# Layer 3 of a four-layer convolution stack: products along h one group ahead, modes with channels innermost

## The chip, the cores and the metric

The kernel runs on one core of a Trainium2 chip. The metric is the device time of one execution in microseconds. The kernel before takes 7563.33 us, the median of three runs (7562.54 to 7565.89). The profile shows one other execution, of 7617.3 us with the profiler on; all times within the kernel below are of that execution, counted from its start.

A core has five engines that run side by side: TensorE multiplies matrices and writes to PSUM, VectorE and ScalarE compute elementwise and carry results from PSUM to SBUF, GpSimd does odd jobs and issues DMAs, SyncE issues DMAs. Each runs its own list of instructions in order and waits on semaphores for the others.

## The reference

The input x has 4 batches of 64 channels of 256 x 256, in fp32. Four layers follow, each a residual over a group norm of 32 groups. The first three are a gated convolution block with a patchwise FFT, a 3 x 3 convolution, and a thresholded convolution. The change is in the fourth, layer 3, which multiplies the low Fourier modes by weights:

```python
def _L3_conv_ref(x, weights1, weights2):
    x_ft = jnp.fft.rfft2(x)
    top = jnp.einsum('bixy,ioxy->boxy', x_ft[:, :, :M1, :M2], w1)
    bot = jnp.einsum('bixy,ioxy->boxy', x_ft[:, :, H - M1:, :M2], w2)
    out_ft = out_ft.at[:, :, :M1, :M2].set(top)
    out_ft = out_ft.at[:, :, H - M1:, :M2].set(bot)
    return jnp.fft.irfft2(out_ft, s=(H, W))
...
x = x + _L3_conv_ref(_gn(x), L3_conv_weights1, L3_conv_weights2)
```

M1 and M2 are 16: of 256 x 129 modes only 32 x 16 are kept, so the transforms are small products with cosine and sine matrices.

## The kernel before

Layer 3 (`_layer3`) has two stages. The first computes the kept modes of all batches, scales them by the group norm and multiplies them by the weights. The second transforms back, adds x and stores. The change is in the first.

A batch b is taken in 16 groups of 4 channels (CC). For each group:

1. `load` brings 4 channels of x, 1 MB, into one of six slots (three tags of two buffers, line 1179). A slot is free for the next load when the products of its group are done.
2. Products along h (line 1220, written `psa`): the 256 rows lie as 2 x 128 on the partitions; four matmuls in the code, eight in the trace, give 64 values for each channel and column: 32 frequencies, real and imaginary. Two PSUM tiles (`ps_a`) serve in turn.
3. ScalarE copies the result to SBUF, tile `a` (line 1225; pool `p_a`, three buffers).
4. Four transposes on TensorE (line 1229, `psat`) bring the columns onto the partitions, in one of two PSUM tiles (`ps_t`).
5. VectorE copies them to `ah`, in two operations (line 1235). `ah` is [128, NW, C, 4M]: for each channel the 64 values stand together. There is one buffer of it.

When a batch is complete, products along w (line 1248, `psx`) contract the columns; they read `ah` with the channels 64 words apart. ScalarE copies the result to `xw` (line 1255). TensorE turns it (line 1261, `psxt`) so that channels are on the partitions, and VectorE writes the modes to `xm`, times the group norm's factor r, in 24 operations (lines 1271 to 1273: for each half s of the frequencies and each of 4 strips k, one operation for the upper 64 partitions and two for the lower, where real and imaginary parts change places and one gets a minus). Two small operations (line 1276) add the mean's part to the zero mode. After the last batch the modes are multiplied by the weights (line 1287, `psm`), which wait for all of `xm`.

In layers 0 to 2 the order of TensorE, VectorE, ScalarE and SyncE is that of the program text (`tc.manual_schedule`). Layer 3 is not in such a block. There a planner orders the instructions of each engine at build time: it goes through them with its own estimates of how long each takes, and of those whose inputs and buffers it believes ready it takes the one that stands first in the program. The chip then runs each list as planned, in order. So the program text decides between instructions that are ready together, and the estimates decide what is ready.

Of the kernel before, what the change touches and what calls it, by code (L numbers as in the profile page):

```python
# [10 lines left out]
F32 = mybir.dt.float32  # L11
U32 = mybir.dt.uint32
AF = mybir.ActivationFunctionType
ALU = mybir.AluOpType
# [3 lines left out]
C = 64  # L18
# [100 lines left out]
class _Net:  # L119
# [1044 lines left out]
    def _layer3(self, ctx, src, dst):  # L1164
        tc, nc, a, B, H, W = self.tc, self.nc, self.a, self.B, self.H, self.W
        pool = lambda c, name, bufs, **k: c.enter_context(tc.tile_pool(name=name, bufs=bufs, **k))
        M = MODES
        NH, NW = H // 128, W // 128
        CC, NK = 4, 2
# [3 lines left out]
        def load(b, c0, name, pool=None):  # L1173
            if pool is None:
                x = self.slot(next(turn) % 3, name).rearrange("p r w -> p (r w)")[:, 0 : CC * NH * W]
                x = x.rearrange("p (c n w) -> p c n w", c=CC, n=NH)
            else:
                x = pool.tile([128, CC, NH, W], F32, tag="x", name=name)
            nc.sync.dma_start(
                x.rearrange("p c n w -> p c (n w)"),  # L1180
                src[b][c0 : c0 + CC].rearrange("c (p n) w -> p c (n w)", n=NH),
            )
            return x

        first = {c0: load(0, c0, f"x3_0_{c0}") for c0 in range(0, NX * CC, CC)}
        cp = pool(ctx, "l3c", 1)
        eh = self.load("c_eh", cp)
        ew = cp.tile([128, NW, 2, 2 * M], F32, name="ew")
# [4 lines left out]
        xm = cp.tile([128, 2, M, M, 2, B], F32, name="xm")  # L1193

        om = cp.tile([128, M, B, 3, M], F32, name="om")
        halves = [slice(0, C), slice(C, 128)]

        with ExitStack() as c2:
            p_w = pool(c2, "l3w", 3)
            p_ah, p_a = pool(c2, "l3ah", 1), pool(c2, "l3a", 3)  # L1200
            ps_a, ps_t = pool(c2, "l3pa", 2, space=PSUM), pool(c2, "l3pt", 2, space=PSUM)
            ps_x, ps_m = pool(c2, "l3px", 1, space=PSUM), pool(c2, "l3pm", 1, space=PSUM)
            wts, xs = {}, {}
            self.small = lambda name: ps_m.tile([128, 512], F32, tag="m", name=name)

            def load_w(k0):
                wt = wts[k0] = p_w.tile([128, 2, NK, M * C], F32, tag="w", name=f"wt_{k0}")
                nc.sync.dma_start(wt, a["wf"][:, :, k0 : k0 + NK])

            for b in range(B):  # L1210

                ah = p_ah.tile([128, NW, C, 4 * M], F32, tag="ah", name=f"ah_{b}")
                for c0 in range(0, C, CC):
                    x = first.pop(c0, None) if b == 0 else None
                    x = xs[b, c0] = x or load(b, c0, f"x3_{b}_{c0}")
                    for c1 in range(0, CC, 4):
                        ps = ps_a.tile([128, 2, W], F32, tag="a", name=f"psa_{b}_{c0}_{c1}")
                        for n in range(NH):
                            for j in range(2):
                                nc.tensor.matmul(  # L1220
                                    ps[halves[j]], eh[:, n, :], x[:, c1 + 2 * j : c1 + 2 * j + 2, n, :],
                                    start=(n == 0), stop=(n == NH - 1),
                                )
                        m = p_a.tile([128, 2, W], F32, tag="m", name=f"a_{b}_{c0}_{c1}")
                        nc.scalar.copy(m, ps)  # L1225
                        pt = ps_t.tile([128, NW, 2, 2, 4 * M], F32, tag="t", name=f"psat_{b}_{c0}_{c1}")
                        for n in range(NW):
                            for k in range(2):
                                nc.tensor.transpose(  # L1229
                                    pt[:, n, k].rearrange("p j f -> p (j f)"),  # L1230
                                    m[:, k, n * 128 : (n + 1) * 128], self.ident,
                                )
                        c = c0 + c1
                        for n in range(NW):
                            nc.vector.tensor_copy(
                                ah[:, n, c : c + 4, :].rearrange("p (j k) f -> p k j f", j=2), pt[:, n]
                            )
                    if c0 % 16 == 0:
                        self.next_norms()
                if b < 3:  # L1240
                    load_w(b * NK)

                psx = ps_x.tile([128, 4, 128], F32, tag="x", name=f"psx_{b}")
                ahv = ah.rearrange("p n c (s g k r) -> p n g r k s c", s=2, g=4, k=4)
                for n in range(NW):
                    for ri in range(2):
                        for g in range(4):
                            nc.tensor.matmul(  # L1248
                                psx[32 * g : 32 * g + 32].rearrange("p k (s c) -> p k s c", s=2),
                                ew[:, n, ri, :], ahv[:, n, g, ri],  # L1250
                                start=(n == 0 and ri == 0), stop=(n == NW - 1 and ri == 1),
                                tile_position=(0, 32 * g),
                            )
                xw = p_a.tile([128, 4, 128], F32, tag="m", name=f"xw_{b}")
                nc.scalar.copy(xw, psx)

                pxt = ps_x.tile([128, 2, 4, 4, 2, M], F32, tag="xt", name=f"psxt_{b}")
                for s in range(2):
                    for k in range(4):
                        for h in halves:  # L1260
                            nc.tensor.matmul(
                                pxt[h, s, k].rearrange("p g r w -> p (g r w)"), xw[:, k, s * C : (s + 1) * C],
                                self.ident, start=True, stop=True,
                            )
                r, nb = self.r[3][:, b : b + 1], self.nb[3][:, b : b + 1]
                up, low = halves
                for s in range(2):
                    xb = xm[:, s, :, :, :, b].rearrange("p (g k) w r -> p k g w r", g=4)
                    for k in range(4):
                        v = pxt[:, s, k].rearrange("p g r w -> p g w r")  # L1270
                        nc.vector.tensor_scalar(xb[up, k], v[up], r[up], None, ALU.mult)
                        nc.vector.tensor_scalar(xb[low, k, :, :, 0], v[low, :, :, 1], r[low], -1.0, ALU.mult, ALU.mult)
                        nc.vector.tensor_scalar(xb[low, k, :, :, 1], v[low, :, :, 0], r[low], None, ALU.mult)
                for k, h in enumerate(halves):
                    dc = xm[h, 0, 0, 0, k, b : b + 1]
                    nc.vector.scalar_tensor_tensor(dc, nb[h], float(H * W), dc, ALU.mult, ALU.add)

            for k0 in range(0, M, NK):
                if k0 + 2 * NK < M and k0 > 0:
                    load_w(k0 + 2 * NK)  # L1280
                wt = wts[k0]
                ps = ps_a.tile([128, 2, W], F32, tag="a", name=f"psm_{k0}").rearrange("p k w -> p (k w)")
                ps = ps[:, 0 : NK * M * 2 * B].rearrange("p (k w r b) -> p k w r b", k=NK, w=M, r=2)
                for k in range(NK):
                    for kw in range(M):
                        for s in range(2):
                            nc.tensor.matmul(
                                ps[halves[s], k, kw].rearrange("p r b -> p (r b)"),
                                wt[:, s, k, kw * C : (kw + 1) * C],
                                xm[:, s, k0 + k, kw].rearrange("p r b -> p (r b)"), start=True, stop=True,  # L1290
                            )
                for k in range(NK):
                    nc.scalar.copy(om[:, :, :, 0:2, k0 + k], ps[:, k].rearrange("p w r b -> p w b r"))
                    nc.vector.tensor_scalar(om[:, :, :, 2, k0 + k], ps[:, k, :, 0, :], -1.0, None, ALU.mult)

        with ExitStack() as c2:
            p_x2, p_z, p_tm = pool(c2, "l3x2", NY), pool(c2, "l3z", 3), pool(c2, "l3t", 2)
            ps_t, ps_z = pool(c2, "l3pt2", 2, space=PSUM), pool(c2, "l3pz", 2, space=PSUM)
# [19 lines left out]
            for i, (b, c0) in enumerate(parts):  # L1318
# [3 lines left out]
                if i < NX:  # L1322
                    x = xs[b, c0]
                else:
                    x = load(b, c0, f"x4_{b}_{c0}", p_x2 if (i - NX) % (NX + NY) < NY else None)
# [53 lines left out]
```

## Time and profile before

| what | value |
|---|---|
| time, median of 3 | 7563.33 us |
| profiled span | 7617.3 us |
| first psa to last psxt of layer 3 | 6976.7 to 7232.7 us |
| products along w start (batches 0 to 3) | 7040.4, 7100.5, 7160.1, 7222.9 us |
| products with the weights (psm) | 7241.3 to 7296 us |
| second stage of layer 3 | to the end |
| psa matmuls, 512 of them | mean 624 ns |
| copy to `a`, 64 | mean 586 ns |
| psat transposes, 256 | mean 290 ns |
| copy to `ah`, 128 | mean 419 ns |
| operations to `xm`, 96 | mean 456, 340, 337 ns |

In the profile PE is TensorE (PEld its loading of weights), DVE VectorE, ACT ScalarE, POOL GpSimd and SP SyncE. A row of the timeline reads: start, length, engine, line, operation, tile written <- tiles read, shape, count, and in brackets how long the engine was idle before it and what ended that. Matmuls overlap in the engine, so a duration is longer than the pace at which they follow each other; the pace is read from their starts. The windows view gives busy time and count of each engine in a stretch, then the granted clock of TensorE (1.00 is full), the busy share of the DMA engines and their GB/s.

### The profile page before, as it was taken

How to read it: one execution, taken by the hardware profiler on the slowest of the kernel's cores; microseconds unless marked ns; L12 is line 12 of the kernel's file. 1: busy time of each engine (PE TensorE's matmuls, PEld its weight loads, DVE VectorE, ACT ScalarE, POOL GpSimd, SP SyncE). 2: the span in 40 equal slices, each digit the busy share in tenths (PEclk: the TensorE clock that was granted, in tenths of full speed). 3: DMA queues.
4: the chain of work that ended last, by engine and by line, in shares of the span. 5: the costliest groups of instructions: out<-in, count | busy, mean ns of one | idle time of the engine just before them, and what ended most of it. 6: DMA issues, size and time to landing. Idle time of an engine off the chain costs nothing. (4 is left out here: it accounts for less than half of the span.)

```text
span 7617.3 us, 398890 instructions
## 1 busy us (share of the span) xinstructions
PE 7303.1 (96%) x189304; PEld 4319.0 (57%) x189304; DVE 6594.7 (87%) x5915; ACT 3659.3 (48%) x3917; POOL 660.3 (9%) x1435
## 2 busy tenths in 40 slices
PE   6999999999999999999999999899989999998797
PEld 4666666666666666666666666433324444443276
DVE  7999999999999999999899899899989888885345
ACT  3445444444444454444444545322238778774111
POOL 0000000000000000000000000001102222221011
PEclk9999999999999999999999999999999999999955
DMA  3222222222222222222111121487766766677789
GB/s 129 62 65 63 63 61 61 59 61 59 61 62 61 59 59 62 62 59 54 45 47 47 46 50 44 100 197 196 195 162 171 178 171 175 171 178 232 243 333 396
DMA packets 651203, 875.63 MB, mean 115 GB/s; under 512 B 44020, under 2 KB 470212, under 8 KB 647524
## 3 DMA queue, kind: packets, MB, share of 16 engines
q1 hardware_dynamic: 568548, 581.61, 28.8%
q0 software_dynamic: 81024, 268.50, 12.1%
q8 instruction: 1485, 24.33, 1.4%
q14 instruction: 146, 1.20, 0.1%
HBM read 581.50 MB, written 268.44 MB: 112 GB/s over the span
## 5 line engine op out<-in xcount | busy, mean ns | idle before, releaser
L462 PE MATMUL psd<-y,diag 32*32 32x512 f32 x73296 | 2547.8, 598 | 16.0 <-issue 14.5
L500 DVE SCALAR_TENSOR_TENSOR v<-y,sb_w_dw,v 128x2048 f32<-128x2048 f32 x1024 | 2391.0, 2335 | 110.3 <-ACT v L498 87.7
L462 PEld LDWEIGHTS psd<-y,diag 32*32 32x32 f32 x73296 | 1524.3, 103 | 877.9 <-issue 366.7
L442 ACT COPY y<-psy 128x512 f32<-128x512 f32 x1536 | 915.4, 659 | 1683.3 <-PE psy L435 1681.2
L400 DVE TENSOR_TENSOR up<-psu,flt 128x768 f32<-128x768 f32 x1024 | 932.4, 951 | 226.6 <-PE psu L397 225.8
L435 PEld LDWEIGHTS psy<-sb_c_bdft,up 64*64 64x64 f32 x49152 | 859.5, 135 | 350.9 <-issue 139.1
L435 PE MATMUL psy<-sb_c_bdft,up 64*64 64x64 f32 x49152 | 931.3, 221 | 32.6 <-issue 29.7
L397 PE MATMUL psu<-win,xf 64*64 64x384 f32 x8192 | 788.5, 487 | 18.5 <-DVE h L482 10.1
L1000 DVE TENSOR_TENSOR q<-xn 128x2313 f32<-128x2313 f32 (+2 forms) x256 | 627.3, 2493 | 1.7 <-ACT xn L236 1.7
L1055 PE MATMUL one<-z,wp 32*32 32x512 f32 x16384 | 592.6, 596 | 20.3 <-issue 15.4
L1001 ACT ACTIVATE q<-q 128x2313 f32<-128x2313 f32 (+2 forms) x256 | 528.9, 2086 | 32.0 <-DVE q L1000 30.7
L476 ACT ACTIVATE h<-psd 128x1024 f32<-128x1024 f32 x258 | 251.3, 1023 | 534.9 <-PE psd L462 534.9
L236 ACT ACTIVATE xn<-x,nb,r 128x1024 f32<-128x1024 f32 (+3 forms) x272 | 488.1, 1798 | 41.5 <-DVE q L1000 23.6
L1055 PEld LDWEIGHTS one<-z,wp 32*32 32x32 f32 x16384 | 366.5, 103 | 228.5 <-issue 87.4
L1014 PE MATMUL div<-q,ones 64*32 64x512 f32 x8192 | 469.0, 597 | 13.6 <-ACT q L1001 9.8
L407 POOL MEMSET y<- 128x22 f32 x384 | 52.2, 137 | 4251.2 <-ACT y L415 3217.2
L397 PEld LDWEIGHTS psu<-win,xf 64*64 64x64 f32 x8192 | 305.6, 134 | 184.6 <-issue 85.2
L1088 POOL DMA_DIRECT2D x<-r x512 | 274.2, 543 | 971.0 <-DVE r L1085 943.6
L809 PE MATMUL m<-t,wk 64*64 64x512 f32 x3072 | 352.5, 588 | 0.0
L809 PE MATMUL m<-t,wg 64*64 64x512 f32 x3072 | 343.5, 591 | 4.5 <-DVE wg L771 4.5
L1014 PEld LDWEIGHTS div<-q,ones 64*32 64x32 f32 x8192 | 153.6, 107 | 321.1 <-issue 256.9
L824 ACT COPY s<-m 128x1024 f32<-128x1024 f32 x64 | 64.8, 1013 | 558.9 <-PE m L809 548.6
(138 smaller groups left out, 7625.2 us busy)
## 6 DMA issues: line engine op xcount, KB each, us to landing
x<-x SPq DMA_DIRECT2D x240, 640.0 KB, 6.3
x<-x SPq DMA_DIRECT2D x122, 1024.0 KB, 10.7
x<-in_x_dram SPq DMA_DIRECT2D x256, 256.0 KB, 3.8
x<-o POOLq DMA_DIRECT2D x128, 512.0 KB, 9.2
r<-x SPq DMA_DIRECT2D x512, 128.0 KB, 4.1
x<-r POOLq DMA_DIRECT2D x512, 128.0 KB, 4.0
out_dram<-x POOLq DMA_DIRECT2D x64, 1024.0 KB, 9.8
r<-in_x_dram SPq DMA_DIRECT2D x248, 256.0 KB, 3.8
```

Source lines behind the costliest of these rows:

```text
L236: self.nc.scalar.activation(dst, src, AF.Identity, bias=self.nb[n][p0:p1, b : b + 1], scale=self.r[n][p0:p1, b : b + 1])
L397: nc.tensor.matmul(ps[halves[n], s, 0:384], xf[t][halves[s], n, 4 * g + k], win[halves[s]], start=True, stop=True)
L400: nc.vector.tensor_mul(ups[t, g][:, :, k, :], ps[:, :, 0:384], flt.broadcast_to([128, 2, 384]))
L435: nc.tensor.matmul(ps[halves[c], n, s, :, k, :], up[halves[n], s, k, i * 128 + c * C : i * 128 + (c + 1) * C], bdft[halves[n]], start=True ...
L442: nc.scalar.copy(yt[t][i][:, 3:11, w0 : w0 + 64].rearrange("p r (k n w) -> p n r k w", k=4, n=2), ps[:, :, s])
L462: ins = nc.tensor.matmul(d[q // 2][quarters[j], q % 2], diag[quarters[q], i, k, :], rows_in(t, i, quarters[q], j, dy)[:, :, dx : dx + W], ...
L500: nc.vector.scalar_tensor_tensor(v, s, wdw[:, 2, k : k + 1], v, ALU.mult, ALU.add)
L809: nc.tensor.matmul(rows2(m)[halves[j], s], gs[i][halves[s], dx, :], ts[n][halves[s], i, 2 * j : 2 * j + 2, dx : dx + W], start=(dx == 0), ...
L1000: nc.vector.tensor_sub(d, p0, p1)
L1001: nc.scalar.activation(d, d, AF.Square)
L1014: ins = nc.tensor.matmul(ps[quarters[j], h], ones[halves[h]], q[n, g, k][halves[h], r + 2 * j : r + 2 * j + 2, o : o + W], start=(m == 0), ...
L1055: ins = nc.tensor.matmul(rows2(ps[g])[quarters[j], k], w[quarters[i]], z[quarters[i], h, 2 * j + dy : 2 * j + dy + 2, dx : dx + W], tile_p ...
```

## The change

The loop over batches becomes three functions and a loop over all 64 groups. `along_h` does steps 1 to 3 of a group, `turned` steps 4 and 5, `along_w` the products along w, `spread` the rest. In each turn i of the loop, `along_h` of group i is given ahead of `turned` of group i − 1. When group i − 1 is the first of a batch, `along_w` of the batch before stands between the two, and `spread` follows `turned`. Its purpose is that TensorE has products to do while ScalarE copies.

`ah` becomes [128, NW, 4M, C], with channels innermost, so that the products along w read neighbouring words; VectorE's copies write with a step of 64 words instead. In PSUM the turned modes are laid out with the strips k inside g, so that one operation can take all four strips: six operations for a batch in place of 24. The weight loads `load_w` come one group earlier in the program. What is computed stays the same.

```diff
-            for b in range(B):
-                ah = p_ah.tile([128, NW, C, 4 * M], F32, tag="ah", name=f"ah_{b}")
...
-                        for n in range(NW):
-                            nc.vector.tensor_copy(
-                                ah[:, n, c : c + 4, :].rearrange("p (j k) f -> p k j f", j=2), pt[:, n]
-                            )
+            ah_of = lambda b: ahs[b].rearrange("p n (s g k r) c -> p n g r k s c", s=2, g=4, k=4)
+            def along_h(b, c0):
...
+            def turned(b, c0):
+                if c0 == 0:
+                    ahs[b] = p_ah.tile([128, NW, 4 * M, C], F32, tag="ah", name=f"ah_{b}")
...
+                for n in range(NW):
+                    nc.vector.tensor_copy(
+                        ahs[b][:, n, :, c0 : c0 + 4].rearrange("p f (j k) -> p k j f", j=2), pt[:, n]
+                    )
...
-                pxt = ps_x.tile([128, 2, 4, 4, 2, M], F32, tag="xt", name=f"psxt_{b}")
+                pxt = ps_x.tile([128, 2, 4, 4, 2 * M], F32, tag="xt", name=f"psxt_{b}")
...
-                                pxt[h, s, k].rearrange("p g r w -> p (g r w)"), xw[:, k, s * C : (s + 1) * C],
-                                self.ident, start=True, stop=True,
+                                pxt[h, s, :, k], xw[:, k, s * C : (s + 1) * C], self.ident, start=True, stop=True
...
-                    xb = xm[:, s, :, :, :, b].rearrange("p (g k) w r -> p k g w r", g=4)
-                    for k in range(4):
-                        v = pxt[:, s, k].rearrange("p g r w -> p g w r")
-                        nc.vector.tensor_scalar(xb[up, k], v[up], r[up], None, ALU.mult)
-                        nc.vector.tensor_scalar(xb[low, k, :, :, 0], v[low, :, :, 1], r[low], -1.0, ALU.mult, ALU.mult)
-                        nc.vector.tensor_scalar(xb[low, k, :, :, 1], v[low, :, :, 0], r[low], None, ALU.mult)
+                    xb = xm[:, s, :, :, :, b]
+                    v = pxt[:, s].rearrange("p g k (r w) -> p (g k) w r", r=2)
+                    nc.vector.tensor_scalar(xb[up], v[up], r[up], None, ALU.mult)
+                    nc.vector.tensor_scalar(xb[low, :, :, 0], v[low, :, :, 1], r[low], -1.0, ALU.mult, ALU.mult)
+                    nc.vector.tensor_scalar(xb[low, :, :, 1], v[low, :, :, 0], r[low], None, ALU.mult)
...
+            groups = [(b, c0) for b in range(B) for c0 in range(0, C, CC)]
+            for i in range(len(groups) + 2):
+                if i < len(groups):
+                    along_h(*groups[i])
+                b, k = divmod(i - 1, NG)
+                if b > 0 and k == 0:
+                    along_w(b - 1)
+                if 0 < i <= len(groups):
+                    turned(*groups[i - 1])
+                if b > 0 and k == 0:
+                    spread(b - 1)
+                if i % NG == NG - 1 and i // NG < 3:
+                    load_w(i // NG * NK)
```

More of the change, by code (lines that the diff above doesn't have):

```diff
@@ L1208, in load_w @@
                 nc.sync.dma_start(wt, a["wf"][:, :, k0 : k0 + NK])
-            for b in range(B):
-                ah = p_ah.tile([128, NW, C, 4 * M], F32, tag="ah", name=f"ah_{b}")
[L1213 to L1222, printed above, removed]
-                                )
-                        m = p_a.tile([128, 2, W], F32, tag="m", name=f"a_{b}_{c0}_{c1}")
-                        nc.scalar.copy(m, ps)
-                        pt = ps_t.tile([128, NW, 2, 2, 4 * M], F32, tag="t", name=f"psat_{b}_{c0}_{c1}")
-                        for n in range(NW):
[L1228 to L1235, printed above, removed]
-                                ah[:, n, c : c + 4, :].rearrange("p (j k) f -> p k j f", j=2), pt[:, n]
[L1237 to L1241, printed above, removed]
@@ new lines, in _layer3 @@
+            NG = C // CC
+            ahs, ms, xws = {}, {}, {}
+            ah_of = lambda b: ahs[b].rearrange("p n (s g k r) c -> p n g r k s c", s=2, g=4, k=4)
+            def along_h(b, c0):
+                x = first.pop(c0, None) if b == 0 else None
+                x = xs[b, c0] = x or load(b, c0, f"x3_{b}_{c0}")
+                ps = ps_a.tile([128, 2, W], F32, tag="a", name=f"psa_{b}_{c0}")
+                for n in range(NH):
+                    for j in range(2):
+                        nc.tensor.matmul(
+                            ps[halves[j]], eh[:, n, :], x[:, 2 * j : 2 * j + 2, n, :],
+                            start=(n == 0), stop=(n == NH - 1),
+                        )
+                m = ms[b, c0] = p_a.tile([128, 2, W], F32, tag="m", name=f"a_{b}_{c0}")
+                nc.scalar.copy(m, ps)
@@ new lines, in turned @@
+            def turned(b, c0):
+                if c0 == 0:
+                    ahs[b] = p_ah.tile([128, NW, 4 * M, C], F32, tag="ah", name=f"ah_{b}")
+                m = ms.pop((b, c0))
+                pt = ps_t.tile([128, NW, 2, 2, 4 * M], F32, tag="t", name=f"psat_{b}_{c0}")
+                for n in range(NW):
+                    for k in range(2):
+                        nc.tensor.transpose(
+                            pt[:, n, k].rearrange("p j f -> p (j f)"), m[:, k, n * 128 : (n + 1) * 128], self.ident
+                        )
+                for n in range(NW):
+                    nc.vector.tensor_copy(
+                        ahs[b][:, n, :, c0 : c0 + 4].rearrange("p f (j k) -> p k j f", j=2), pt[:, n]
+                    )
+                if c0 % 16 == 0:
+                    self.next_norms()
@@ L1243, in _layer3, with along_w @@
+            def along_w(b):
                 psx = ps_x.tile([128, 4, 128], F32, tag="x", name=f"psx_{b}")
-                ahv = ah.rearrange("p n c (s g k r) -> p n g r k s c", s=2, g=4, k=4)
                 for n in range(NW):
@@ L1249, in _layer3 @@
                                 psx[32 * g : 32 * g + 32].rearrange("p k (s c) -> p k s c", s=2),
-                                ew[:, n, ri, :], ahv[:, n, g, ri],
+                                ew[:, n, ri, :], ah_of(b)[:, n, g, ri],
                                 start=(n == 0 and ri == 0), stop=(n == NW - 1 and ri == 1),
@@ L1253, in _layer3, with spread @@
                             )
-                xw = p_a.tile([128, 4, 128], F32, tag="m", name=f"xw_{b}")
+                xw = xws[b] = p_a.tile([128, 4, 128], F32, tag="m", name=f"xw_{b}")
                 nc.scalar.copy(xw, psx)
-                pxt = ps_x.tile([128, 2, 4, 4, 2, M], F32, tag="xt", name=f"psxt_{b}")
+            def spread(b):
+                xw = xws.pop(b)
+                pxt = ps_x.tile([128, 2, 4, 4, 2 * M], F32, tag="xt", name=f"psxt_{b}")
                 for s in range(2):
```

## The prediction

> **What bounds the kernel now.** I read the page first: TensorE is busy 96% of the span, but that is a mean over four layers. The change touches layer 3, the last 640 us, so I went on to the waits between 6972 and 7250 us (engine and line, what it waited for, total us, times, longest).
>
> ```profile
> ACT a L1225 <- PE psa L1220: 167.3, 62, 5.2
> DVE ah L1235 <- PE psat L1229: 131.7, 54, 4.7
> PEld psat L1229 <- ACT a L1225: 96.0, 59, 2.4
> PE psat L1229 <- ACT a L1225: 43.5, 57, 2.3
> DVE xm L1271 <- PE psxt L1261: 39.1, 4, 10.0
> ```
>
> ScalarE and VectorE wait for TensorE, and TensorE waits 57 times (43.5 us) for ScalarE's copy. No row has TensorE waiting for a DMA: the loads keep up. One group of four channels in the timeline (start us, us, engine, line) shows the loop:
>
> ```profile
> 7003.08 0.66 PE L1229 MATMUL psat<-sb_c_ident,a 128*128 128x128 f32 x4 [0.72 <-ACT a L1225]
> 7003.66 0.20 PEld L1220 LDWEIGHTS psa<-x,sb_c_eh 128*64 128x64 f32 x4 [0.17 <-issue]
> 7003.66 1.94 PE L1220 MATMUL psa<-x,sb_c_eh 128*64 128x512 f32 x8
> 7003.77 0.76 DVE L1235 COPY ah<-psat 128x256 f32<-128x256 f32 x2 [2.49 <-PE psat L1229]
> 7005.69 0.59 ACT L1225 COPY a<-psa 128x512 f32<-128x512 f32 x1 [2.66 <-PE psa L1220]
> 7006.32 0.66 PE L1229 MATMUL psat<-sb_c_ident,a 128*128 128x128 f32 x4 [0.72 <-ACT a L1225]
> ```
>
> It is a chain of products, copy, transposes with almost nothing of the next group in the gap: 7003.08 to 7006.32 is 3.24 us a group. The last batch's end is a second serial stretch:
>
> ```profile
> 7222.91 7.06 PE L1248 MATMUL psx<-ah,ew 128*32 128x512 f32 x32 [0.52 <-DVE ah L1235]
> 7230.08 0.59 ACT L1255 COPY xw<-psx 128x512 f32<-128x512 f32 x1 [8.40 <-PE psx L1248]
> 7230.72 1.97 PE L1261 MATMUL psxt<-sb_c_ident,xw 128*64 128x128 f32 x32 [0.75 <-ACT xw L1255]
> 7232.74 0.43 DVE L1271 TENSOR_SCALAR xm<-psxt,r 64x128 f32<-64x128 f32 x1 [9.55 <-PE psxt L1261]
> 7240.83 0.34 DVE L1276 SCALAR_TENSOR_TENSOR xm<-nb,xm 64x1 f32<-64x1 f32 x2
> 7241.32 20.87 PE L1287 MATMUL psm<-xm,wt 128*64 128x8 f32 x388 [8.63 <-DVE xm L1276]
> ```
>
> TensorE stands still 8.63 us while VectorE scales the modes. Last, what the loads could do at most, in three stretches of the windows view (clock, DMA share and GB/s are the last columns; the first two are the steady loop and the stage after, where loads and stores run together):
>
> ```profile
> 7112.00:7160.00 48.00, 38.02 (x182) 14.18 (x182) 18.29 (x54) 8.79 (x15) 0.00 (x0) 1.00 1.01 348
> 7340.00:7350.00 10.00, 8.65 (x51) 6.56 (x43) 6.35 (x11) 1.21 (x2) 1.51 (x2) 0.50 1.04 415
> 7100.00:7112.00 12.00, 11.27 (x75) 3.36 (x74) 1.92 (x7) 1.17 (x2) 0.00 (x0) 1.00 0.27 97
> ```
>
> A DMA share near 1 is not yet the limit: 348 GB/s and 415 GB/s both read as full. While psx runs (third row), the DMA nearly stops because all six slots of x are full. The 3.25 us at which loads are issued is TensorE's pace.
>
> [...] the psa matmuls start two at a time every 0.43 us, so eight take 1.71 us. [...] in the trace it falls in the 8.63 us gap (1.00 until 7234, 0.50 from 7235). [...] the L1235 copies take 419. [...] L1271 takes 440 ns for 128 elements and L1272 340 for 64 (medians), 1.56 ns an element where dense rows take 1.04 (681 ns for 512 on L1345, 1214 for 1024 on L482).
>
> **The change, part by part.**
>
> *Order of products and transposes.* The products along h of group i+1 now stand ahead of the transposes of group i. Nothing of this stage is in a hand-ordered block, so a planner decides; it goes by program order among what it believes ready. It already ran ahead where it could: in the trace two psa matmuls of the following batch stand ahead of psx, and after a psx a run of 20 psa matmuls goes before transposes. So I expect psa(i+1), psat(i), psa(i+2) on TensorE. The buffers allow it: psa has two PSUM tiles and the copy of group i−1 is long done; the copied tile has three; the loads have six slots. The copy's 0.59 us plus its hand-overs then lie beside 1.71 us of products. A group costs 1.71 + 0.58 (from the first transpose to the next psa, 7003.08 to 7003.66) = 2.29 us instead of 3.24, with 0.95 saved.
>
> A batch: 16 x 2.29 + 6.83 (32 psx matmuls at 213.5 ns) + 1.75 (psxt) = 45.2 us. Before, psx starts at 7040.4, 7100.5, 7160.1 and 7222.9, so batches take 60.1, 59.6 and 62.8: savings 14.9, 14.4 and 17.6. The first batch gains less: ScalarE's first copy waits until 6989.2 whatever the order (the idle there is put down to a DMA, 24.0 us), the clock is half until 6996, and psx now has one more group's products in front: about 11 us. Sum 57.9.
>
> *Can the loads follow?* TensorE would ask 1 MB each 2.29 us, 458 GB/s, more than was ever held. Behind a 2 MB weight load at 7139 the trace has loads landing every 2.61 us (five spacings between 7155 and 7168). A batch needs 16 x 2.61 = 41.8 us of transfer within its 45.2. Starting with six full slots, 36.6 us of groups consume 16 and bring 13 or 14, so some 3 stay in hand, which psx refills. Three weight loads of 2 MB cost 5.2 us each, two slots' worth: tight, with some 2 us lost over the stage. I also allow 2 us for hand-overs that I don't see: 57.9 − 4 = about 54 us, with 57 at best.
>
> *Modes with channels innermost.* The psx matmuls now read c at step 1 instead of 64 words, but they already start at 213.5 ns[...]: nothing gained. The L1235 copies now write every element 256 bytes from the last. No row shows this copy; L1294[...] takes 266 ns against 159 for the two-element copies, 1.74 ns an element. So a copy costs between 419 (no penalty) and 158 + 256 x 1.74 = 603 ns. I take 600: 1.2 us of VectorE a group within 2.29, and behind psx's data only at the batch's end, where the next group's 1.71 us of products hides it. Only in the last batch are 0.4 us exposed.
>
> *6 operations for 24.* Now the 24 and two small ones take 8.4 us from the first start to the last end (7232.74 to 7241.17). Then, per s, one of 512 elements and two of 256. At 1.56 ns an element and the intercept of the two rows (240 ns): 1040 + 2 x 640, twice, plus 0.3 = 4.9 us. At 1.04 ns: 770 + 2 x 506, twice, plus 0.3 = 3.9. I take 4.6: 3.8 us saved in the last batch, where psm waits for it. In the first three it lies beside products and only frees VectorE sooner. The strip order in PSUM (32-word pieces) costs psxt nothing I can see: 1.75 us is the weight loads' pace. [...] psm still runs at half clock.
>
> *Moved:* weight loads one group earlier, the norm steps with the transposes: both off the path.
>
> Sum: 54 + 3.8 + 2 of small relief after each psx (VectorE holds the first transposes of batches 1 to 3 for about 0.7 us) = 60 us. The stage after is limited by its transfers (415 GB/s, share 1.04), but these begin only once psm is done and its space is free, so it moves forward whole. 7563.3 − 60 = 7503 us.
>
> **The rivals.**
>
> *Loads bind.* For it: share about 1 in the steady loop, and a landing median of 7.0 us, 5.2 at least. If three in flight sustain only 350 GB/s, 3.0 us a load, a batch is 48 us of loads plus weights, and the saving falls to about 40 + 4: 7519. Against: 2.61 us under backlog.
>
> *The planner keeps its order.* If it thinks x late, transposes still go first, and only the 6-for-24 and the relief remain, some 6 us: 7557. Against: the two matmuls it already puts ahead.
>
> *Slower.* If the 256-byte writes cost 1.8 us a copy, two are 3.6 us a group and VectorE sets the pace: 64 x 0.36 = 23 us more, 7586. The same comes out if the transposes land straight behind their own products, with the 0.43 us that now hides part of the copy lost: 64 x 0.43 − 4 = 23. Against: no strided row above costs over 1.74 ns an element.
>
> **How the numbers follow.** Main case 0.73, loads bind 0.15, order kept 0.07, slower 0.05. The forecast is the main case. The range 7490 to 7528 holds it with copies free of penalty and no stall (lower end) and the loads at 3.0 us (upper end with some 9 us over), and leaves out the last two. Faster by over 0.2% (15 us): 0.73 + 0.15 = 0.88; within: 0.07; slower: 0.05.
>
> **What would show it.** In the profile after: psat not waiting for ACT a any more; groups every 2.3 us; psx starts some 45 us apart; psa waiting for a DMA only for single microseconds; ah copies near 600 ns; six operations a batch in xm's three lines and the gap ahead of psm near 5 us. Wrong if groups stay at 3.2 us (order), or if they sit at 2.6 to 3.0 with waits for x (loads), or if VectorE is busy throughout (writes).

## The result and the profile after

The changed kernel takes 7531.81 us (median of four runs, 7522.21 to 7539.59) where the kernel before takes 7564.61 (four runs, 7562.54 to 7572.59): a ratio of 0.9954, with a 95% interval of 0.9937 to 0.9971. It is faster, by 33 us. The forecast was 60 us (7503), with a range up to 7528 that misses the result by 4 us.

I call *the stage* the stretch from the first psa to the first psm, the part that the change touches. It was 264.6 us (6976.7 to 7241.3) and is 228.6 (6917.9 to 7146.5): 36.0 us less. Layers 0 to 2 are the same program and yet differ from one execution to the next (layer 3 begins at 6976.7 and at 6917.9 in these two), so the stage is the sharper measure below. From the first psm to the end it is 376.0 us before and 374.0 after.

The windows view of the kernel after, cut at the four starts of psx and at the first psm (stretch, us, busy us and count of PE, PEld, DVE, ACT and POOL, granted clock, DMA share, GB/s):

```profile
6917.90:6970.60 52.70, 47.29 (x211) 17.95 (x211) 24.19 (x49) 9.27 (x16) 5.29 (x10) 0.88 1.03 385
6970.60:7024.80 54.20, 47.12 (x258) 17.69 (x256) 21.48 (x40) 9.95 (x17) 0.00 (x0) 1.00 0.95 326
7024.80:7077.90 53.10, 45.36 (x250) 17.22 (x248) 21.04 (x40) 9.95 (x17) 0.00 (x0) 1.00 0.95 332
7077.90:7134.60 56.70, 45.54 (x256) 17.23 (x256) 21.50 (x41) 9.85 (x17) 0.00 (x0) 1.00 0.62 224
7134.60:7146.50 11.90, 5.61 (x64) 2.69 (x65) 5.29 (x9) 0.58 (x1) 0.00 (x0) 0.96 0.01 2
```

Batches 1 to 3, forecast at 45.2 us, last 54.2, 53.1 and 56.7. TensorE is busy only 45 to 47 us of each, and the last batch has a DMA share of 0.62: it isn't the loads that fill it. The waits of the same kernel say what does (engine and line, what it waited for, us, times, longest):

```profile
PEld psat L1236 <- ACT a L1226: 58.1, 40, 2.1
PE psat L1236 <- ACT a L1226: 27.6, 40, 2.0
PEld psat L1236 <- issue: 21.3, 26, 0.9
```

The transposes still wait for ScalarE's copy 40 times; 26 times only their weight load waits, for nothing that the profile shows ("issue"). Counted in TensorE's timeline, 25 of the 64 groups run in the intended order, with the next group's products ahead of their transposes. The timeline shows both kinds. In batch 0:

```profile
6954.24 0.65 PE L1236 MATMUL psat<-sb_c_ident,a 128*128 128x128 f32 x4
6954.41 0.58 ACT L1226 COPY a<-psa 128x512 f32<-128x512 f32 x1 [1.87 <-PE psa L1221]
6954.83 1.94 PE L1221 MATMUL psa<-x,sb_c_eh 128*64 128x512 f32 x8
6956.69 0.42 PEld L1236 LDWEIGHTS psat<-sb_c_ident,a 128*128 128x128 f32 x4 [0.81 <-issue]
6956.70 0.66 PE L1236 MATMUL psat<-sb_c_ident,a 128*128 128x128 f32 x4
```

and in batch 2:

```profile
7053.10 0.58 ACT L1226 COPY a<-psa 128x512 f32<-128x512 f32 x1 [2.68 <-PE psa L1221]
7053.74 0.66 PE L1236 MATMUL psat<-sb_c_ident,a 128*128 128x128 f32 x4 [0.74 <-ACT a L1226]
7054.32 1.94 PE L1221 MATMUL psa<-x,sb_c_eh 128*64 128x512 f32 x8
7056.36 0.58 ACT L1226 COPY a<-psa 128x512 f32<-128x512 f32 x1 [2.68 <-PE psa L1221]
7057.00 0.66 PE L1236 MATMUL psat<-sb_c_ident,a 128*128 128x128 f32 x4 [0.74 <-ACT a L1226]
```

In batch 0 the copy ends (6954.99) long before the transposes that read it (6956.70), with a group of products between: a group each 2.46 us (6954.24 to 6956.70). In batch 2 each copy is followed at once by its own transposes: 3.26 us (7053.74 to 7057.00), as before the change. The planner goes back to the old order within each batch, though the program text does not: the intended order holds for the first 14 groups of batch 0, for the first 5 of batch 1, for the first 5 of batch 2, and for one group of batch 3.

The end of the last batch, in the same timeline:

```profile
7134.65 3.64 PE L1252 MATMUL psx<-ah,ew 128*32 128x512 f32 x32 [0.68 <-DVE ah L1240]
7138.69 0.58 ACT L1259 COPY xw<-psx 128x512 f32<-128x512 f32 x1 [5.43 <-PE psx L1252]
7139.33 1.97 PE L1268 MATMUL psxt<-sb_c_ident,xw 128*64 128x128 f32 x32 [1.04 <-ACT xw L1259]
7141.35 1.11 DVE L1276 TENSOR_SCALAR xm<-psxt,r 64x512 f32<-64x512 f32 x1 [6.32 <-PE psxt L1268]
7146.02 0.34 DVE L1281 SCALAR_TENSOR_TENSOR xm<-nb,xm 64x1 f32<-64x1 f32 x2
7146.50 1.74 PE L1308 MATMUL psm<-xm,wt 128*64 128x8 f32 x29 [5.21 <-DVE xm L1281]
```

The 32 psx matmuls take 3.64 us where they took 7.06, and the gap ahead of psm is 5.21 where it was 8.63.

### The profile page after: what moved, and what is told of

It is laid out like the page before. It is cut to its first block, busy times and chain, and to the rows that moved or that the text cites. A ratio compares the mean times of both kernels' runs of the same rounds, so it can differ in the third digit from the quotient of the medians.

```text
span 7520.5 us, 398811 instructions
## 1 busy us (share of the span) xinstructions
PE 7250.4 (96%) x189304; PEld 4323.5 (57%) x189304; DVE 6598.8 (88%) x5843; ACT 3655.1 (49%) x3917; POOL 659.1 (9%) x1435
## 5 line engine op out<-in xcount | busy, mean ns | idle before, releaser
L1001 ACT ACTIVATE q<-q 128x2313 f32<-128x2313 f32 (+2 forms) x256 | 529.1, 2086 | 32.7 <-DVE q L1000 31.2
```

Of the source, the lines that this page charges most:

```text
L1001: nc.scalar.activation(d, d, AF.Square)
```

## The experiments

My theory after the result, **the order**: the planner reckons with the loads of x coming late, puts a group's own transposes ahead of products that it believes not ready, and so gives back most of the gain; the transfers themselves could follow. The rival, **the transfers**: x arrives too slowly, so a better order would only wait for x. The runs of the first table are from one chip, where the kernel before takes 7599.08 us, those of the second from another, where it takes 7584.31; the last, of the copies alone, is on its own.

| kernel | time, us | stage, us | batches 0 to 3, and the end, us |
|---|---|---|---|
| before | 7599.08 (profile of 7617.3) | 264.6 | 63.7, 60.1, 59.6, 62.8, 18.4 |
| order by hand | 7545.81 | 207.1 | 57.2, 49.3, 46.7, 42.1, 11.8 |
| channels innermost alone | 7583.64 | 252.4 | 63.5, 57.3, 56.8, 59.8, 15.0 |
| order alone, by hand | 7571.63 | 233.4 | 56.5, 55.8, 52.7, 49.8, 18.6 |
| six operations alone | 7599.75 | 263.5 | 62.9, 61.8, 61.4, 62.4, 15.0 |

| kernel | time, us | stage, us | batches 0 to 3, and the end, us |
|---|---|---|---|
| the changed kernel again | 7559.11 | 230.4 | 54.4, 54.3, 53.1, 56.8, 11.8 |
| half the loads, planner | 7523.29 | 199.4 | 54.6, 45.2, 45.3, 42.6, 11.7 |
| half the loads, by hand | 7516.72 | 198.3 | 54.8, 44.8, 44.9, 42.1, 11.7 |
| by hand, weights last | 7517.62 | 199.5 | 56.0, 44.8, 44.8, 42.2, 11.7 |

Times of kernels without an interval below are single runs, and say little: on the first chip eleven runs of the kernel before lie between 7581.48 and 7607.44. A stage is that of one traced execution each. The two traces of the changed kernel show how far it can be trusted: 228.6 and 230.4 us, with the whole difference in batch 0 (52.7 and 54.4), while batches 1 to 3 and the end agree to 0.1 us. A batch here ends where its psx starts (starts rounded to 0.1 us), so a batch's psx and operations to `xm` count in the next column. By hand batch 0 is a little longer than the planner's (56.0 against 54.4); I did not follow that up.

### The order by hand

```diff
+            by_hand = tc.manual_schedule(
+                engines={
+                    mybir.EngineType.PE, mybir.EngineType.DVE, mybir.EngineType.Activation, mybir.EngineType.SP
+                }
+            )
+            with by_hand:
-            for i in range(len(groups) + 2):
+                for i in range(len(groups) + 2):
...
```

> The changed kernel with its loop over groups in a block ordered by the program text, so that each group's products along h stand ahead of the transposes of the group before in all four batches. Measure: time from the first psa to the first psm in the trace (before 264.6 us, changed kernel 228.6 us), and the whole time. Theory O (the planner, taking x for late, put the transposes straight behind their own products in most of batches 1 to 3, and that is what the gain lacks): groups of 2.45 us throughout, batches about 45 us, stage about 200 us, whole time about 28 us under the changed kernel's 7532, near 7504. Rival L (the chip's loads would not have kept up anyway): TensorE waits for x in batches 1 to 3, batches of 50 us or more, stage 215 us or more, whole time within 12 us of the changed kernel's.

The same instructions, in the order of the program text: 7545.81 us (six runs, 7532.46 to 7551.71), ratio 0.9932 (0.9919 to 0.9945). The stage is 207.1 us, 21.5 less than in the changed kernel and 57.5 less than before. The 207.1 are 7 us more than theory O expected (about 200), with batches of 49.3, 46.7 and 42.1 where it had about 45, and well under the 215 of rival L; by the ratios to the kernel before (0.9932 and 0.9954) the whole time gains some 17 us on the changed kernel, where 28 were expected. The block fixes the order of VectorE, ScalarE and SyncE along with that of TensorE; they weren't tried apart. All groups but the last one have the intended order now: 62 times only the transposes' weight load waits, for nothing that the profile shows. So the transfers could follow, nearly. What they cost is in the second of these rows of its waits:

```profile
PEld psat L1236 <- issue: 52.0, 62, 1.6
PE psa L1221 <- DMA x<-x: 5.7, 4, 2.8
```

### Channels innermost alone

```diff
-                ah = p_ah.tile([128, NW, C, 4 * M], F32, tag="ah", name=f"ah_{b}")
+                ah = p_ah.tile([128, NW, 4 * M, C], F32, tag="ah", name=f"ah_{b}")
...
-                                ah[:, n, c : c + 4, :].rearrange("p (j k) f -> p k j f", j=2), pt[:, n]
+                                ah[:, n, :, c : c + 4].rearrange("p f (j k) -> p k j f", j=2), pt[:, n]
...
-                ahv = ah.rearrange("p n c (s g k r) -> p n g r k s c", s=2, g=4, k=4)
+                ahv = ah.rearrange("p n (s g k r) c -> p n g r k s c", s=2, g=4, k=4)
```

> The kernel before with nothing of the change but the channels innermost in ah (order, 24 operations and PSUM strips as before). Theory S (the step of 64 words in the moving operand halved the pace of the psx matmuls): psx takes about 3.6 us in place of 7.0 in each batch, stage 264.6 - 4 x 3.4 = 251 us; the copies to ah take 600 ns in place of 419 and cost under 1 us in all. Rival I (psx only looks shorter in the changed kernel because it is dealt out between psa matmuls): psx stays at 7.0 us, stage 264 to 266 us.

The stage is 252.4 us, 12.2 less than before, and the groups by line show where it comes from (group, shape and count, busy us and mean ns of one, idle before). Of the kernel before:

```profile
L1248 PE MATMUL psx<-ah,ew 128*32 128x512 f32 x128 | 28.2, 1034 | 1.0 <-DVE ah L1235 1.0
```

and with the new `ah` alone:

```profile
L1248 PE MATMUL psx<-ah,ew 128*32 128x512 f32 x128 | 14.6, 595 | 1.4 <-DVE ah L1235 1.4
```

128 matmuls take 14.6 us instead of 28.2, which is 13.6 us over the stage, or 3.4 a batch, and batches 1 to 3 and the end are each some 3 us shorter (2.8, 2.8, 3.0 and 3.4). Only the layout of what they read differs. Theory S had it so: 3.6 us a batch and a stage of 251 us were expected.

### The order alone, by hand

The order by hand, with the old `ah` and the 24 operations.

```diff
-            ah_of = lambda b: ahs[b].rearrange("p n (s g k r) c -> p n g r k s c", s=2, g=4, k=4)
+            ah_of = lambda b: ahs[b].rearrange("p n c (s g k r) -> p n g r k s c", s=2, g=4, k=4)
...
-                    xb = xm[:, s, :, :, :, b]
+                    xb = xm[:, s, :, :, :, b].rearrange("p (g k) w r -> p k g w r", g=4)
+                    for k in range(4):
...
```

> The order by hand as in the first run, but ah with the 64 values innermost, the PSUM strips and the 24 operations as before. If the order is worth what theory O says and adds to the layout: groups of 2.45 us, psx of 7.0 us, batches of 48 to 49 us, a gap of 8.6 us ahead of psm, stage 200 + 4 x 3.4 + 4 = 218 us. If VectorE's 8.4 us of operations behind each psx hold up the transposes once the order is tight: 3 us more a batch, 227 us. If loads bind: no faster than 225 us with TensorE waiting for x.

The stage is 233.4 us, above the 218 and the 227 that were expected. It is also over the 225 of the rival that the loads bind, but TensorE's products wait for x only 4.5 us in all, less than by hand with all three parts (5.7). The order by itself brings 31.2 of the 57.5 that the three parts bring by hand. Against the run with all three, batches 1 to 3 are 6.5, 6.0 and 7.7 us longer. The slower psx is 3.4 of each. For the remaining 2.6 to 4.3 the waits have a row that the run with all three hasn't, one stop of TensorE in each of batches 1 to 3 (the waits for x fall differently in the two runs, so the difference isn't the price of the stop alone):

```profile
PE psat L1236 <- DVE ah L1240: 8.5, 3, 2.8
```

The first of the three in the timeline, after a psx:

```profile
7034.43 0.32 DVE L1283 SCALAR_TENSOR_TENSOR xm<-nb,xm 64x1 f32<-64x1 f32 x2
7034.76 1.41 DVE L1240 COPY ah<-psat 128x256 f32<-128x256 f32 x4
7035.66 1.09 PE L1236 MATMUL psat<-sb_c_ident,a 128*128 128x128 f32 x4 [2.82 <-DVE ah L1240]
7036.68 3.68 PE L1221 MATMUL psa<-x,sb_c_eh 128*64 128x512 f32 x8
```

VectorE is at the 24 operations and the two small ones for 8.5 us (7026.27 to 7034.75); both psat tiles are full until it copies them; TensorE stands 2.82 us, and then a group of products takes 3.68 us instead of 1.94: the granted clock is 0.50 from 7035.7 to 7041.3, by the windows view. The stop of batch 3 (2.82 us, until 7144.16) is followed by slower products too, 3.25 us for the group; that of batch 2 (2.81 us, until 7091.43) is not, and its group takes 1.94. With groups one ahead, this hold of VectorE (8.5 us) stops TensorE.

### Six operations alone

```diff
-                pxt = ps_x.tile([128, 2, 4, 4, 2, M], F32, tag="xt", name=f"psxt_{b}")
+                pxt = ps_x.tile([128, 2, 4, 4, 2 * M], F32, tag="xt", name=f"psxt_{b}")
...
-                    for k in range(4):
...
+                    nc.vector.tensor_scalar(xb[up], v[up], r[up], None, ALU.mult)
+                    nc.vector.tensor_scalar(xb[low, :, :, 0], v[low, :, :, 1], r[low], -1.0, ALU.mult, ALU.mult)
+                    nc.vector.tensor_scalar(xb[low, :, :, 1], v[low, :, :, 0], r[low], None, ALU.mult)
```

> The kernel before with nothing of the change but the six operations for 24 and the PSUM strips that they need. Expected: the gap ahead of psm falls from 8.63 to about 5.2 us (the three lines took 1132, 693 and 664 ns in the changed kernel), 3.4 us of the stage, and 0 to 2 us more from transposes that wait less behind each psx: stage 259 to 261 us. Rival: nothing beyond the gap, and the planner's order shifts: 264 us or more.

The end is 3.4 us shorter, as expected, and yet the stage is 263.5 us, above the expected 259 to 261: it loses only 1.1 us, since batches 1 and 2 are 1.7 and 1.8 us longer. TensorE in the timeline of the kernel before, after its first psx:

```profile
7055.01 0.66 PE L1229 MATMUL psat<-sb_c_ident,a 128*128 128x128 f32 x4 [0.72 <-ACT a L1225]
7055.60 4.59 PE L1220 MATMUL psa<-x,sb_c_eh 128*64 128x512 f32 x20
7060.12 1.18 PE L1229 MATMUL psat<-sb_c_ident,a 128*128 128x128 f32 x8
```

and with the six operations:

```profile
7037.09 0.66 PE L1229 MATMUL psat<-sb_c_ident,a 128*128 128x128 f32 x4 [0.72 <-ACT a L1225]
7037.68 1.94 PE L1220 MATMUL psa<-x,sb_c_eh 128*64 128x512 f32 x8
7040.34 0.65 PE L1229 MATMUL psat<-sb_c_ident,a 128*128 128x128 f32 x4 [0.72 <-ACT a L1225]
```

The 20 products in a row, then 8 transposes without a wait, were a piece of the good order that the planner had found by itself; they stand where VectorE is at its 24 operations (until 7059.1, and until 7037.9 with the six). With the six the planner puts the transposes first, and the wait of 0.72 us returns. That it does so because it reckons with VectorE free sooner is my reading.

### Half the loads, in the planner's hands and by hand

Every second group reads the x of the group before, apart from the last six groups (and the first six, whose loads are given earlier), so that half of the loads of x are left out in batches 1 and 2, and 26 of the 64 in all. The same edit in the changed kernel and in the one by hand:

```diff
+                if c0 // CC % 2 and (b, c0) not in [(B - 1, c) for c in range(C - NX * CC, C, CC)]:
+                    x = x or xs[b, c0 - CC]
                 x = xs[b, c0] = x or load(b, c0, f"x3_{b}_{c0}")
```

> The changed kernel in the planner's hands, but every second group of four channels takes the x of the group before it instead of loading its own, so half of layer 3's loads along h are left out (the output is of other data). Theory P (the planner puts the transposes straight behind their own products because it reckons with x arriving late): with half the loads it has no such reason, the products of the next group stand ahead all through, groups take 2.45 us in every batch, and the first products to the first mode product take about 200 us (228.6 after). Theory L (the transfers themselves keep the groups slow): also about 200 us, but then the run by hand with half the loads is as far below the run by hand with all of them. Theory R (another reason for the planner's order: buffers, priorities): the order stays mixed, groups of 3.26 us remain in batches 1 to 3, about 222 to 228 us.

> The order by hand, with the same half of the loads left out. In the run by hand with all loads some 8 us of waits for x were left in the 207.1 us from the first products to the first mode product. Theory P (the order, not the transfers, held the changed kernel back): about 199 us, only those 8 us less. Theory L (the transfers held it back): much less than 199 us, 190 or under, since then the groups of 2.45 us would also shrink towards 2.29.

In the planner's hands the stage falls from 230.4 to 199.4 us, by hand to 198.3. The planner now keeps the intended order in 63 of 64 groups; its timeline of TensorE in batch 2:

```profile
7057.26 0.65 PE L1238 MATMUL psat<-sb_c_ident,a 128*128 128x128 f32 x4
7057.84 1.94 PE L1223 MATMUL psa<-x,sb_c_eh 128*64 128x512 f32 x8
7059.71 0.66 PE L1238 MATMUL psat<-sb_c_ident,a 128*128 128x128 f32 x4
7060.30 1.94 PE L1223 MATMUL psa<-x,sb_c_eh 128*64 128x512 f32 x8
```

Groups of 2.45 us, no wait for a copy. So what made it leave that order was the loads. And by hand, leaving these loads out is worth only 207.1 − 198.3 = 8.8 us: that is what the transfers cost there, while the planner's order costs 228.6 − 207.1 = 21.5. What the planner takes a load to last isn't in any profile; since each x then also stands in its slot for two groups, "the loads" is here the loads together with the slots that they fill. Nor was the planner's order tried with more slots, or with the loads of weights elsewhere.

### The weights last

```diff
-                    if i % NG == NG - 1 and i // NG < 3:
-                        load_w(i // NG * NK)
+                    if i == len(groups) - 1:
+                        for k0 in range(0, 3 * NK, NK):
+                            load_w(k0)
```

> The order by hand, with the three first weight loads of 2 MB given after the last load of x instead of one at the end of each of the first three batches. Theory W (each weight load makes the x behind it land about 5 us later, and that is the waits for x left in the run by hand): those waits, some 8 us, go; the first products to the first mode product take about 200 us instead of 207, and the ratio to the kernel before is about 0.9923 (0.9932 by hand without this). Theory N (the waits come from the pace of the x loads alone, 2.65 us against 2.45): nothing gained or 2 us at most, 0.9930; and if the weights come too late, psm waits for them and it is slower than that.

> The changed kernel itself on the chip of these runs, so that the versions by hand are compared with it and not only with the kernel before: 0.9954 of the time before, and 0.002 to 0.003 above the version with the weights last if theory P and W hold; no difference beyond 0.001 if the order by hand was worth nothing.

By hand with the weights last: 7517.62 us (four runs, 7513.37 to 7524.32), ratio 0.9909 (0.9894 to 0.9924). The changed kernel in the same runs: 7559.11 (five runs), 0.9964 (0.9951 to 0.9976). The intervals lie apart, by 0.0055 where 0.002 to 0.003 was expected: some 40 us, of which 30.9 are the stage and the rest lies outside it, unexplained. Of the kernels timed in several runs and with all loads this one is the best; against the order by hand with the weights between (0.9919 to 0.9945) the intervals overlap, so that the weights' part is shown by the stage and the waits, not by the time. Its windows:

```profile
7002.80:7047.60 44.80, 44.63 (x258) 17.12 (x256) 21.59 (x40) 9.98 (x17) 0.00 (x0) 1.00 1.01 369
7047.60:7092.40 44.80, 44.63 (x258) 17.12 (x256) 21.63 (x40) 9.97 (x17) 0.00 (x0) 1.00 1.03 375
7092.40:7134.60 42.20, 41.13 (x246) 16.19 (x245) 21.09 (x40) 9.38 (x16) 0.00 (x0) 1.00 1.02 383
7134.60:7146.30 11.70, 5.58 (x64) 2.63 (x64) 5.24 (x9) 0.59 (x1) 0.00 (x0) 0.89 0.44 182
```

TensorE is busy all of batches 1 and 2, with all loads there and a DMA share of 1.01 to 1.03, and no row of its waits has psa waiting for x. The weights use the DMA in the last row, where it was idle (0.44, before 0.01), and psm doesn't wait for them. In the run with the weights between, the first x behind a weight load had waited for it; its timeline at the end of batch 1 shows the price:

```profile
7049.04 0.65 PE L1236 MATMUL psat<-sb_c_ident,a 128*128 128x128 f32 x4
7052.50 2.94 PE L1221 MATMUL psa<-x,sb_c_eh 128*64 128x512 f32 x8 [2.80 <-DMA x<-x]
7055.36 1.11 PE L1236 MATMUL psat<-sb_c_ident,a 128*128 128x128 f32 x4
```

2.80 us of waiting, and then products and transposes at a lower clock (2.94 and 1.11 us instead of 1.94 and 0.65; the mean clock is 0.60 from 7052.5 to 7056.4).

### The copies to ah, written four words at a time

```diff
-                        ahs[b][:, n, :, c0 : c0 + 4].rearrange("p f (j k) -> p k j f", j=2), pt[:, n]
+                        ahs[b][:, n, :, c0 : c0 + 4].rearrange("p f (j k) -> p f j k", j=2), pt[:, n].rearrange("p k j f -> p f j k")
```

> The order by hand with the weights last, and the two copies to ah of each group written in another order: channels innermost, so four neighbouring words at a time go into ah and the reads in PSUM step by 32 words, where so far each write is 64 words from the last and the reads are dense. Theory S (the step of the writes costs the copies their 600 ns against 419 before): copies near 419 ns. Theory E (any order that isn't dense on both sides costs about that much): 600 ns or more. Either way the time stays within 2 us of the version with the weights last, since VectorE has 1.2 us of work in a group of 2.45.

By the groups by line:

```profile
L1240 DVE COPY ah<-psat 128x256 f32<-128x256 f32 x128 | 48.1, 419 | 110.6 <-PE psat L1236 110.5
```

419 ns, as before the change, where writes 64 words apart take 600 on the same data. The reads in PSUM step by 64 and 128 words in this kernel (not by 32, as I had written), and that costs nothing here. The stage is 198.3 us (199.5 without), and one run takes 7495.68 beside 7565.90 for one of the kernel before on that chip: within what was expected, since VectorE isn't what a group waits for.

## Why the prediction was wrong

The direction was right, the mechanism of the gain too; the forecast of 60 us met 33. Point by point:

**The order: the step that failed.** "So I expect psa(i+1), psat(i), psa(i+2) on TensorE." That came in 25 of 64 groups. I had the clue in hand twice: I wrote that the planner goes by what it *believes* ready, and I named as a rival that it might think x late. I gave that 0.07, because in the trace x was never waited for, and took two early matmuls for proof. But a trace shows when x came, not when the planner thought it would. Of the rival, too, the size was off: I took it as all or nothing (7557), and what came was a mixture. That the loads, or the slots that they fill, turn the planner back is shown: with 26 of the 64 left out it keeps the order by itself. That it does so by taking x for late fits this, and fits that the order comes back after each of the first two psx, which give loads time; the planner's own reckoning wasn't seen. The bill: batches 1 to 3 are 9.4, 8.3 and 14.5 us longer than by hand with the weights last, 32.2 in all. In 32 of their groups the transposes wait the full 0.74 us for their copy, and 32 times 3.26 − 2.45 = 0.81 us is 26 of it.

**The first batch.** "About 11 us": 63.7 to 52.7, right.

**A group at 2.29 us.** Mis-sized: 2.45 wherever the order holds. I added 1.71 of products and 0.58 from the first transpose to the next product; the 0.16 that is missing lies between the last pair of products and the transposes, whose weight load stands 0.81 us ("issue") until the products are through: from 6954.83 to 6956.69 it is 1.86, not 1.71. Over 64 groups 10 us. It went unseen because before the change a wait for the copy lay there in nearly every group. The run of 20 products that I cited has none, and could have warned me: 4.52 us (7055.60 to 7060.12) where 20 at 213.5 ns make 4.27, though the profile puts the wait of the weight load behind it down to VectorE.

**Modes with channels innermost: "nothing gained".** Wrong, and by luck near the size of the last error with the other sign: 3.4 us a batch against 2.6. I took the pace of the psx matmuls (213.5 ns) for a limit, since the psa matmuls on as many columns keep the same pace; no trace had shown it to be one. It was a mean over matmuls that run side by side: psx started four at a time every 0.86 us, psa two at a time every 0.43, so that 213.5 ns was not the pace of one matmul. With neighbouring words psx starts four at a time every 0.43 us. Each old one also took 1034 ns from start to end, against 624 for a psa matmul on as many columns, and that was the sign that reading held them up. With the layout alone changed each takes 595. With both errors a batch by hand is 44.8 us, and I had 45.2.

**The copies to ah.** 600 ns taken, 600 measured; hidden beside the products, as said. The 600 was an estimate from L1294 (266 ns), whose 64 writes are 48 words apart. The step of the writes is the cause (419 with four words at a time).

**Six operations for 24.** In the last batch 3.8 us forecast, 3.4 measured (8.63 to 5.21): near, though the three forms take 1132, 693 and 664 ns, above both of my bounds (770 to 1040 and 506 to 640). "2 of small relief after each psx" was right in neither order: with the planner's, the six operations alone make batches 1 and 2 longer by 1.7 and 1.8 us, and with the order by hand the 24 stop TensorE for 2.8 us in each of batches 1 to 3 (order alone), and after two of these stops eight products take 3.68 and 3.25 us instead of 1.94.

**Can the loads follow?** Yes: in batches 1 and 2 with the weights last there is no wait for x at 44.8 us a batch. "Some 2 us lost" to weight loads was too low: 7.6 us (207.1 against 199.5, traces of two chips), of which 5.7 are waits for x; behind the longest of them, of 2.80 us, the clock was low as well (0.60 in the mean). The rival that the loads bind (7519 us) is closest to the measured time and yet not what happened.

**The stage after moves forward whole, psm at half clock.** Both right: psm takes 54.8 us at a clock of 0.50 in both, and the rest 321.2 and 319.2. The granted clock fell within the gap of 5.21 us (1.00 from 7144 to 7145, 0.50 from 7145.5), as it had within that of 8.63.

The sum of the forecast, 60, is near what the change is worth with its order kept and the weights out of the way, 264.6 − 199.5 = 65.1 us, but partly by luck: 13.6 of these are the faster psx, which the forecast had at nothing. What the changed kernel lacks is the order.

What stays open: why the planner turns back after 14 groups of batch 0, after 5 of batches 1 and 2 and almost at once in batch 3, whether it is the loads' length or their slots that it goes by, and what in TensorE makes the transposes' weight load wait 0.81 us; none was tried apart.

## What to carry to other kernels

Where a planner orders the instructions, a change of program order is a request. Ask what it believes of each input's arrival, above all of loads, and don't take the trace's punctual data for its belief; after the change, count in the waits how many groups have the new order before explaining anything else. If the order matters and the transfers can follow, write it by hand, and then put long loads that nobody needs yet behind the short ones that somebody does. And the price of a step depends on the order around it: six operations for 24 lengthened two batches by 1.7 and 1.8 us in one order, and in the other took away a stop of 2.8 us a batch.

## What the runs showed of the hardware

- A read of their moving data from SBUF with a step of 64 words halves the pace of the psx matmuls: 128 take 28.2 us so and 14.6 with neighbouring words (1034 and 595 ns each), with nothing else of them changed.
- VectorE's copy of 256 words from PSUM takes 600 ns if each write is 64 words from the last, and 419 if four at a time are neighbours, though the reads then step by 64 and 128 words. It was the writes that cost, not the reads.
- A stop of TensorE of 2.8 us can be enough to lower its clock, and isn't always. Of four such stops in batches 1 to 3 of two kernels three were followed by slower products (3.68, 3.25 and 2.94 us for eight instead of 1.94; the granted clock was 0.50 from 7035.7 to 7041.3 behind the first of them, and 0.60 in the mean from 7052.5 to 7056.4 behind the last), and one, of 2.81 us, was not: 1.94 us. In the kernel before, ahead of this stage, the clock behind a stop of 2.44 us was 0.50 (6880.3 to 6883.3), and behind one of 2.52 us it was 1.00 (6795.9 to 6800.0).
- With the weights last, a DMA share of 1.01 to 1.03 at 369 to 383 GB/s held for three batches without a product waiting for x.
